# Moving the norm of the first batch half, its gates and one block product among the attention steps of a fused fp32 transformer kernel

## The chip, the cores and the metric

One core of a Trainium2 chip runs the whole program in one launch. The metric is device time in microseconds (us), the median of three runs. Five engines work side by side: TensorE (PE, matmuls and transposes), VectorE (DVE), ScalarE (ACT), GpSimd (POOL) and SyncE (SP), whose queue here issues most of the DMA transfers. Each executes its own instructions in order and waits on semaphores for the others.

## What is computed

The input `x` has 2 batch elements of 512 tokens with 1024 features; all arithmetic is fp32. Two layers follow, each with two residual steps:

```python
x = x + fake_quant_product(layernorm(x), ctx)        # layer 0
x = x + linear_with_mixed_lora(layernorm(x))         # layer 0
x = x + cross_attention(layernorm(x), ctx, ctx)      # layer 1: 32 heads, 8 kv heads, head size 128
x = x + ffn(layernorm(x))                            # layer 1
```

The cross attention has 1024 context positions, rotary embedding, a mask, a softmax and an output projection `wo` (4096 to 1024). The last step, which the change moves, is

```python
logits = h @ gate_w.T + expert_bias                  # h = layernorm(x), 4 experts
one_hot = jax.nn.one_hot(jnp.argmax(logits, -1), 4)
z = jnp.einsum('nh,erh->ner', h, lora_A)             # rank 8
delta = jnp.einsum('neh,ne->nh', jnp.einsum('ner,ehr->neh', z, lora_B), one_hot)
x = x + h @ W_up.T + delta
```

## The kernel before

The program is one long list of instructions written by Python generators; each `next()` emits a stretch of one of them, and that is how stages are interleaved. TensorE always runs in the order in which the program is written (L977). In the attention loop (L1123 to L1149) DVE, ACT and POOL do so too; behind it, and for SP throughout, a scheduler chooses the order. Tiles come from pools: `u8` (8 KB a partition, 14 buffers), `u4`, `u2`, `small` in SBUF; in PSUM `wide` with two buffers and `b` with four. A transfer or an operation into a tile waits until the earlier user of its buffer is done.

**Products.** The large products use one level of the Strassen-Winograd scheme: seven block products in place of eight, with sums of the operand blocks made before (`left_sums`, `right_sums`, L229 to L276, on DVE or, for attention's output, on POOL: L245 to L253; for weights L259, L262, L264, L267) and of the results after (`seven_onto`: L316, L317, L320 on DVE, L322 on POOL). The matmuls of all of them are recorded at L347.

**Attention.** `attention` (L836 to L927) takes one head per step, 64 heads (the first 32 belong to batch 0), with three phases a step that work on different heads:

- phase 0: scores of head n+2 (L748) and the addition of the mask by DVE (L762); loads of the next head's q and, every fourth step, of kT and v (`begin`) through SP;
- phase 1: the finished head is normalized by POOL (L822); every fourth step POOL forms the operand sums of a finished group of four heads; three or four stretches of the output projection of the group before (L347 with L317, L320, L322), which adds into the rows of `x`; the tree of maxima (L770 to L776);
- phase 2: the sum of the exponentials is turned (`turn_sum`, PE at L712, DVE at L714, L785), two halves of the product with v (`attend`, L811), and the exponentials of head n+1 (DVE L794, ACT L797, then POOL L800, L803, L804, L805, which add up the denominators).

The rows of `x` of one batch element lie in two 1 MB tiles (`halves`). They were stored to DRAM by `put_away` (L1087) earlier and are fetched again when the projection of that batch element begins (L873). Batch 0's projections end around step 36; its rows then lie unused until the last steps.

**The norm.** `all_moments` (L179) makes the statistics of a batch element, one quarter of 128 rows per `next` (BNStats, L163, and aggregation, L164), then one Sqrt on ACT (L186), then a reciprocal (L188). `scaled` (L166) subtracts and multiplies on DVE. `transposed` (L200) turns 128 rows: eight PE transposes into a `wide` PSUM tile (L204), two copies to SBUF by ACT (L205) and DVE (L206).

**Gates.** `gated` (L930) multiplies the turned rows with 36 columns (4 gate logits, 32 columns of `lora_A`): 8 matmuls for each of four quarters (L939), into two `b` tiles; each appears as two records in the profile. DVE then takes maxima and a mask per quarter (L950 to L957), POOL clears the tile for two quarters (L960), DVE multiplies (L962); PE turns the result (L972), DVE copies it (L973). It is the additional operand of four of the seven products of `linear` (L562).

**The end.** In the last five attention steps the statistics, scaling and turning of batch 0 are interleaved; the gates of batch 0 follow as one run of matmuls, the weights `W_up` are loaded and summed (`matrix`, L544), and the seven products of both row blocks follow, mixed with what is left of attention. Then batch 1 is normed among the last products of batch 0 (`weave`), its gates follow as one run, then its products and the stores of the output (L1171, L1180).

Of the kernel before, what the change touches and what calls it, by code (L numbers as in the profile page):

```python
# [39 lines left out]
def decoder_kernel(  # L40
# [300 lines left out]
    def advance(stretches, n):  # L341
        for _ in range(n):
            next(stretches)
# [585 lines left out]

    def gated(quarters):  # L930

        zT, diff = u2([P, S]), u2([P, 256])
        gaccs = []
        for t in range(NT):
            if t % 2 == 0:
                gacc2 = ps_b((P, 2, 256))
            gacc = gacc2[:, t % 2]
            for c in range(NC):
                nc.tensor.matmul(  # L939
                    gacc[:, :NGA],  # L940
                    chunk(quarters, c, t),
                    ga_t[:, c, :],
                    start=(c == 0),
                    stop=(c == NC - 1),
                )
            gaccs.append(gacc)
        zs = []
        for t, gacc in enumerate(gaccs):
# [12 lines left out]
            z = z2[:, t % 2]  # L961
            nc.vector.tensor_tensor(  # L962
                z[:, : E1 * R1].rearrange("p (e r) -> p e r", r=R1),
                gacc[:, E1:NGA].rearrange("p (e r) -> p e r", r=R1),
                lg.unsqueeze(2).to_broadcast([P, E1, R1]),
                ALU.mult,
            )
            zs.append(z)
        yield
        tr = ps_tr()  # L970
        for t, z in enumerate(zs):
            nc.tensor.transpose(tr[:, t, :], z, ident)  # L972
        nc.vector.tensor_copy(zT, tr.rearrange("p t n -> p (t n)"))  # L973
        yield split_tokens(zT, diff)
# [143 lines left out]
                w = quad_weights(wq, q + 1)  # L1118


    extra = {-2: 3, -1: 2, 0: 2, 1: 2, 2: 2, 3: 2, 4: 1}
    steps = attention({**extra, "products": main, "later": later})
    with tc.manual_schedule(  # L1123
        engines={
            mybir.EngineType.DVE,
            mybir.EngineType.Activation,
            mybir.EngineType.Pool,
        }
    ):
        for _ in range(3 * (B * NH - 5)):  # L1130
            next(steps)
        stats = all_moments(0)
        for _ in range(NT):
            for _ in range(2):
                next(steps)
            ready = next(stats)
            next(steps)
        next(steps)
        next(stats)
        next(steps)  # L1140
        next(stats)
        hs, norms = normed(0, u8, 2, ready)
        next(norms)
        next(steps)

    for _ in range(2):
        next(steps)
        for _ in range(2):
            next(steps)  # L1149
            next(norms)  # L1150
    gates = gated(hs)
    next(gates)
    for _ in range(2):
        next(steps)
    zTs = [next(gates), None]
    bl_t = u4([P, D])
    nc.sync.dma_start(bl_t, bl1T)
    w_ops = matrix(wupT, u8, 4)
    main = linear(0, token_sums(hs, lambda: u4([P, 4, 256])), w_ops, lambda: zTs[0], bl_t)
    advance(main, 4)  # L1160
    for _ in range(3):
        next(steps)
# [12 lines left out]
    advance(main, 2)  # L1175
    zTs[1] = next(gates)
# [75 lines left out]
```

## Time and profile before

| what | value |
|---|---|
| median of 3 runs | 2507.97 us (2507.82 to 2508.96) |
| the profiled execution | 2505.61 us |
| its span in the profile | 2503.8 us |
| mean granted TensorE clock | 0.989 |
| instructions | 19692 |
| attention step, start of scores to start of the next, four in mid-run | 21.55, 19.82, 21.92, 19.83 us |
| the same with the statistics in it, near the end | 22.47, 20.70, 22.33, 20.71 us |
| POOL's last addition to batch 0's rows ends | 1759.8 us |
| loads of kT, v, q around there are issued, and their data used | 1750.9 us, 1778.3 us |
| a 1 MB store of rows, and a 1 MB fetch, issue to landing | 3.9 us, 6.3 us |

How to read the profile: the row of busy shares gives each engine's busy time, the share of the span, and its records. A timeline line has the start, the length, the engine, the line of the kernel, the operation, the output and its inputs by pool, shapes, the count of like records in a row, and in brackets the idle time before it and who ended it. A row of waits has the engine and line that waited, the line waited for, the total, the count and the longest. A window row has the stretch, its length, busy time and records of each engine, the granted clock of TensorE (1.00 is full speed), the mean busy share of the DMA engines, and GB/s.

### The profile page before, as it was taken

Reading aid. Unit: us, or ns where it says so; the run is one execution under the profiler, and the core shown is the slowest. Engines: PE = TensorE matmul, PEld = TensorE weight load, DVE = VectorE, ACT = ScalarE, POOL = GpSimd, SP = SyncE. Lnnn points to the kernel's source line nnn. Section 1 sums busy time; section 2 is a strip of 40 time slices with the busy share of each in tenths; the row PEclk is TensorE's granted clock in tenths of the full one; section 3 lists DMA queues with packets and bytes.
Section 4 is the critical chain, followed back from the end, with each engine's and each line's share of the span. In section 5 each row is a group of like instructions: output and inputs, shape, how many; then the busy total and the mean of one; then the engine's idle time right before and its main releaser. Section 6 shows DMA issues by size and latency. Waiting matters only on the chain. (4 is left out here: it accounts for less than half of the span.)

```text
span 2503.8 us, 19692 instructions
## 1 busy us (share of the span) xinstructions
PE 2441.2 (97%) x6848; PEld 1218.0 (49%) x6856; DVE 1851.0 (74%) x2036; ACT 527.7 (21%) x615; POOL 1006.5 (40%) x536
## 2 busy tenths in 40 slices
PE   7999999999999998989999999999999999998998
PEld 3477458654444443434444444444444444444453
DVE  5848764346886547888888888888888888896451
ACT  1201221011122222222222222222222222223000
POOL 0000010111000001567677767776777667666121
PEclk8999999999999999999999999999999999999899
DMA  7225232013894221244323332443234323333100
GB/s 263 105 94 196 85 120 102 21 67 109 296 336 174 80 97 58 80 126 114 93 80 93 114 94 83 123 147 96 82 88 114 102 75 88 114 93 108 52 34 34
DMA packets 147379, 277.54 MB, mean 111 GB/s; under 512 B 29200, under 2 KB 47136, under 8 KB 146256
## 3 DMA queue, kind: packets, MB, share of 16 engines
q1 hardware_dynamic: 107024, 235.96, 28.1%
q10 hardware_dynamic: 39824, 39.60, 6.6%
q8 instruction: 55, 0.90, 0.1%
q0 software_dynamic: 432, 0.71, 0.1%
q14 instruction: 44, 0.36, 0.1%
HBM read 217.24 MB, written 58.98 MB: 110 GB/s over the span
## 5 line engine op out<-in xcount | busy, mean ns | idle before, releaser
L347 PE MATMUL b<-u,u 128*128 128x512 f32 (+1 forms) x3648 | 1416.6, 546 | 23.5 <-DVE u L291 10.0
L347 PEld LDWEIGHTS b<-u,u 128*128 128x128 f32 x3648 | 694.2, 192 | 710.8 <-issue 623.6
L748 PE MATMUL wide<-u,u 128*128 128x512 f32 x1024 | 455.3, 595 | 17.2 <-DVE small L714 8.5
L811 PE MATMUL b<-u,u 128*128 128x512 f32 x1024 | 461.3, 593 | 0.0
L800 POOL TENSOR_TENSOR u<-u 128x1024 f32<-128x1024 f32 x64 | 151.5, 2367 | 735.8 <-DMA row<-small 383.9
L762 DVE TENSOR_TENSOR u<-wide,u 128x1024 f32<-128x1024 f32 x256 | 312.7, 1224 | 129.0 <-PE wide L748 129.0
L797 ACT ACTIVATE u<-u 128x2048 f32<-128x2048 f32 x128 | 244.7, 1912 | 695.3 <-DVE u L794 633.9
L748 PEld LDWEIGHTS wide<-u,u 128*128 128x128 f32 x1024 | 193.0, 190 | 268.3 <-issue 175.4
L794 DVE TENSOR_TENSOR u<-u,b 128x2048 f32<-128x2048 f32 x128 | 290.3, 2268 | 0.0
L322 POOL TENSOR_TENSOR u<-u,u 128x512 f32<-128x512 f32 x120 | 185.5, 1564 | 228.3 <-DVE u L320 213.5
L811 PEld LDWEIGHTS b<-u,u 128*128 128x128 f32 x1024 | 186.7, 192 | 185.2 <-issue 185.2
L320 DVE TENSOR_TENSOR u<-u,b 128x512 f32<-128x512 f32 x200 | 135.9, 680 | 140.8 <-PE b L347 140.8
L803 POOL TENSOR_TENSOR u<-u,u 128x1024 f32<-128x1024 f32 x64 | 150.7, 2355 | 37.8 <-ACT u L797 37.6
L804 POOL TENSOR_TENSOR u<-u,u 128x1024 f32<-128x1024 f32 x64 | 150.8, 2356 | 4.9
L822 POOL TENSOR_TENSOR u<-u,u 128x512 f32<-128x512 f32 x64 | 119.8, 1871 | 16.0 <-DMA u<-row 16.0
L1054 POOL DMA_DIRECT2D u<-in_b_dram x1 | 0.6, 561 | 301.5 <-PE wide L450 301.5
L216 ACT ACTIVATE u<-u 64x512 f32<-64x512 f32 x72 | 45.2, 628 | 343.2 <-DVE u L293 166.9
L770 DVE TENSOR_TENSOR u<-u 128x1024 f32<-128x1024 f32 x64 | 115.6, 1806 | 0.0
L712 PEld LDWEIGHTS wide<-ident,u 128*128 128x128 f32 x512 | 80.4, 203 | 70.9 <-issue 56.6
L772 DVE TENSOR_TENSOR u<-u,u 128x1024 f32<-128x1024 f32 x64 | 105.8, 1654 | 0.2
L805 POOL TENSOR_TENSOR u<-u 128x512 f32<-128x512 f32 x64 | 100.2, 1566 | 4.9
L774 DVE TENSOR_TENSOR u<-u,u 128x1024 f32<-128x1024 f32 x64 | 97.0, 1515 | 0.2
(124 smaller groups left out, 1553.9 us busy)
## 6 DMA issues: line engine op xcount, KB each, us to landing
u<-row ACTq DMA_DIRECT2D x128, 256.0 KB, 3.7
u<-wo SPq DMA_DIRECT2D x64, 512.0 KB, 3.9
u<-in_wo_dram SPq DMA_DIRECT2D x48, 512.0 KB, 4.6
u<-in_wq_dram SPq DMA_DIRECT2D x32, 512.0 KB, 4.1
q<-u SPq DMA_DIRECT2D x64, 256.0 KB, 2.1
u<-in_wo_dram SPq DMA_DIRECT2D x16, 1024.0 KB, 7.9
wo<-u SPq DMA_DIRECT2D x32, 512.0 KB, 3.9
u<-q SPq DMA_DIRECT2D x64, 256.0 KB, 4.2
```

The lines of the kernel that those rows point to most:

```text
L320: nc.vector.tensor_tensor(c, c, acc, ALU.add)
L322: nc.gpsimd.tensor_tensor(c, c, u, ALU.add)
L347: nc.tensor.matmul(acc, lhsT, rhs, start=start and k == 0, stop=k == len(pairs) - 1, skip_group_check=True,)
L748: nc.tensor.matmul(sc[:, ts(n, HALF)], self.kT[:, ts(2 * j + n, P)], self.qT, start=True, stop=True,)
L762: nc.vector.tensor_tensor(self.e[j // 2][:, js, :], sc.rearrange("p (k q) -> p k q", k=2), mask[j], ALU.add)
L794: nc.vector.tensor_tensor(e, e, self.nmf.unsqueeze(1).to_broadcast([P, 4, S]), ALU.add)
L797: nc.scalar.activation(e, e, AF.Exp)
L800: nc.gpsimd.tensor_tensor(d, e[:, 0:2, :], e[:, 2:4, :], ALU.add)
L803: nc.gpsimd.tensor_tensor(d, d, e[:, 0:2, :], ALU.add)
L804: nc.gpsimd.tensor_tensor(d, d, e[:, 2:4, :], ALU.add)
L811: nc.tensor.matmul(self.acc, self.v[:, k, :], self.e[j][:, k % 4, :], start=(k == 0), stop=(k == NKT - 1),)
L822: nc.gpsimd.tensor_tensor(self.oT, self.oT, self.den, ALU.mult)
```

## The change

- The statistics of batch 0 move from steps 57 to 61 to steps 38 to 42 (`all_moments(0)`, one quarter in phase 1 of steps 38 to 41, the Sqrt in phase 0 of step 42, the reciprocal in phase 1).
- In step 42 the two row tiles of batch 0 are stored to DRAM through SP, and their buffers are given up; two `u8` tiles for the turned rows are taken.
- In steps 44 and 48 one half of the rows (1 MB) is fetched again into one `u8` tile; the four quarters are scaled in steps 45, 46, 49, 50 (in place, in the fetched tile) and turned in steps 46, 47, 50, 51.
- In step 61 two quarters of `W_up` are loaded, and the rows are fetched back. All gate matmuls of batch 0 stand in phase 1 of step 62, in one run, and write one `wide` PSUM tile in place of two `b` tiles; DVE's part and the loads of the other two weight quarters in phase 2; the turning of its result and the first of the seven products, for both row blocks, in phase 1 of step 63. The loop with a written-out order on DVE, ACT and POOL now runs to the end of step 63.
- `token_sums` and `right_sums` follow, then two phases of attention, then five more stretches of products.
- For batch 1 the gate matmuls of a quarter (8) stand directly behind the turning of the next quarter, and each such pair between products of batch 0, in place of one run of 32 after all four.

```diff
     def gated(quarters):
         zT, diff = u2([P, S]), u2([P, 256])
-        gaccs = []
+        gaccs = ps_wide().rearrange("p (t n) -> p t n", t=NT)
         for t in range(NT):
-            if t % 2 == 0:
-                gacc2 = ps_b((P, 2, 256))
-            gacc = gacc2[:, t % 2]
             for c in range(NC):
                 nc.tensor.matmul(
-                    gacc[:, :NGA],
+                    gaccs[:, t, :NGA],
...
                 )
-            gaccs.append(gacc)
+            yield
...
+    stats = all_moments(0)
+    last = {"zT": [None] * B, "w": [None] * 7, "h": [None] * 7}
+
+    def turn_away():
+        last["ready"] = next(stats)
+        put_away(0)
+        hs = [u8([P, 4, S]) for _ in range(2)]
+        last["hs"] = [[hs[ch][:, :, ts(th, 256)] for ch in range(2)] for th in range(2)]
+
+    def fetch_half(i):
+        last["rows"] = u8([P, 2, D])
+        nc.sync.dma_start(last["rows"], x_d[0][i])
+
+    def scale_row(t):
+        mean, rstd = last["ready"][t]
+        r = last["rows"][:, t % 2, :]
+        nc.vector.tensor_scalar(r, r, mean, rstd, ALU.subtract, ALU.mult)
+
+    def turn_row(t):
+        transposed(
+            last["rows"][:, t % 2, :],
+            [last["hs"][t // 2][j][:, :, ts(t % 2, P)] for j in range(2)],
+        )
...
+    def fetch_rows():
+        x[0] = halves()
+        for t, d in zip(x[0], x_d[0]):
+            nc.sync.dma_start(t, d)
+
+    def begin_map():
+        hs = last["hs"]
+        last["h"][:2] = hs[0]
+        last["gates"] = gated(hs)
+
+    hooks = {(42, 0): [lambda: next(stats)], (42, 1): [turn_away]}
+    for t in range(NT):
+        hooks[(38 + t, 1)] = [lambda: next(stats)]
+    for i in range(2):
+        n = 44 + 4 * i
+        hooks[(n, 2)] = [lambda i=i: fetch_half(i)]
+        hooks[(n + 1, 1)] = [lambda i=i: scale_row(2 * i)]
+        hooks[(n + 2, 1)] = [lambda i=i: turn_row(2 * i), lambda i=i: scale_row(2 * i + 1)]
+        hooks[(n + 3, 1)] = [lambda i=i: turn_row(2 * i + 1)]
+    hooks[(61, 2)] = [
+        lambda: fetch_weight(1, 0, 0),
+        lambda: fetch_weight(2, 1, 0),
+        fetch_rows,
+        begin_map,
+    ]
+    hooks[(62, 1)] = [lambda: advance(last["gates"], 4)]
+    hooks[(62, 2)] = [
+        lambda: next(last["gates"]),
+        lambda: fetch_weight(7, 0, 1),
+        lambda: fetch_weight(3, 1, 1),
+    ]
...
-        for _ in range(3 * (B * NH - 5)):
+        for i in range(3 * (B * NH + 2)):
             next(steps)
-        stats = all_moments(0)
-        for _ in range(NT):
-            for _ in range(2):
-                next(steps)
-            ready = next(stats)
-            next(steps)
...
-        hs, norms = normed(0, u8, 2, ready)
-        next(norms)
-        next(steps)
-
+            n, phase = divmod(i, 3)
+            for act in hooks.get((n - 2, phase), ()):
+                act()
+            if (n - 2, phase) == (63, 1):
+                zTs = [next(last["gates"]), None]
+                h_ops, parts = last["h"], last["w"]
+                w_ops = lambda i, c: parts[i - 1][:, c, :]
+                bl_t = u4([P, D])
+                nc.sync.dma_start(bl_t, bl1T)
+                main = linear(0, h_ops, w_ops, lambda: zTs[0], bl_t)
+                advance(main, 2)
...
-    gates = gated(hs)
-    next(gates)
-    for _ in range(2):
-        next(steps)
-    zTs = [next(gates), None]
-    bl_t = u4([P, D])
-    nc.sync.dma_start(bl_t, bl1T)
-    w_ops = matrix(wupT, u8, 4)
-    main = linear(0, token_sums(hs, lambda: u4([P, 4, 256])), w_ops, lambda: zTs[0], bl_t)
-    advance(main, 4)
-    for _ in range(3):
+    h_ops[:] = token_sums(last["hs"], lambda: u4([P, 4, 256]))
+    for _ in range(2):
         next(steps)
-    advance(main, 3)
+    parts[:] = right_sums(
+        nc.vector, parts[0], parts[6], parts[1], parts[2], lambda: u8([P, 4, HALF])
+    )
+    advance(main, 5)
     for _ in steps:
         pass
     hs, norms = normed(1, u4, 4)
-    weave(main, norms, 1, 2)
-    for _ in norms:
+    gates = gated(hs)
+
+    def turned_and_gated():
+        next(norms)
+        yield
+        next(norms)
+        yield
+        for _ in range(3):
+            next(norms)
+            next(gates)
+            yield
+        next(gates)
+        yield
+        next(gates)
+        yield
+
+    side = turned_and_gated()
+    weave(main, side, 1)
+    for _ in side:
         pass
     for t in range(NT):
         nc.sync.dma_start(out[0, ts(t, P), :], rows(0, t))
-    gates = gated(hs)
-    next(gates)
```

More of the change, by code (lines that the diff above doesn't have):

```diff
@@ L945, in gated @@
                 )
-            gaccs.append(gacc)
+            yield
         zs = []
-        for t, gacc in enumerate(gaccs):
+        for t in range(NT):
+            gacc = gaccs[:, t, :]
             lg = small([P, E1])
@@ L1122, in decoder_kernel, with fetch_weight @@
     steps = attention({**extra, "products": main, "later": later})
+    stats = all_moments(0)
[17 more added lines that the diff above has]
+        )
+    def fetch_weight(i, ch, nh):
+        t = last["w"][i - 1] = u8([P, 4, HALF])
+        nc.sync.dma_start(
+            t,
+            wupT[ts(ch, 4 * P), ts(nh, HALF)].rearrange("(c p) n -> p c n", p=P),
+        )
[8 more added lines that the diff above has]
+    hooks = {(42, 0): [lambda: next(stats)], (42, 1): [turn_away]}
+    for t in range(NT):
+        hooks[(38 + t, 1)] = [lambda: next(stats)]
[17 more added lines that the diff above has]
+    ]
     with tc.manual_schedule(
@@ L1129, in decoder_kernel @@
     ):
[L1130 removed]
+        for i in range(3 * (B * NH + 2)):
             next(steps)
[L1132 to L1144 removed]
+            n, phase = divmod(i, 3)
[10 more added lines that the diff above has]
+    h_ops[:] = token_sums(last["hs"], lambda: u4([P, 4, 256]))
     for _ in range(2):
         next(steps)
[L1148 to L1163 removed]
+    parts[:] = right_sums(
+        nc.vector, parts[0], parts[6], parts[1], parts[2], lambda: u8([P, 4, HALF])
+    )
+    advance(main, 5)
     for _ in steps:
```

## The prediction, made before the changed kernel was run

> **What bounds the kernel now.** I read the page's busy shares first, then PE's waits after 2150 us, then PE's timeline from 2280 us on, then windows cut at the clock's edges.
>
> ```profile
> PE 2441.2 (97%) x6848; PEld 1218.0 (49%) x6856; DVE 1851.0 (74%) x2036; ACT 527.7 (21%) x615; POOL 1006.5 (40%) x536
> ...
> PEclk8999999999999999999999999999999999999899
> ```
>
> TensorE is busy for 97% of the span and is the bound. A change that leaves its matmuls alone can only win where PE stands or where its clock falls. The clock row has two dips: at the start and in the third slice from the end (2316 to 2441 us), which this change rebuilds. The waits of PE there:
>
> ```profile
> PE wide L712 <- POOL u L805: 6.8, 1, 6.8
> PE b L972 <- DVE u L962: 5.9, 3, 3.2
> ...
> PE b L347 <- DVE u L267: 0.8, 1, 0.8
> ```
>
> PE's timeline shows where they stand and which groups take longer than the same group elsewhere:
>
> ```profile
> 2280.18 7.05 PE L347 MATMUL b<-u,u 128*128 128x512 f32 x16
> 2287.06 1.04 PE L204 MATMUL wide<-ident,u 128*128 128x128 f32 x8
> 2294.89 1.13 PE L712 MATMUL wide<-ident,u 128*128 128x128 f32 x4 [6.79 <-POOL u L805]
> 2295.81 8.06 PE L811 MATMUL b<-u,u 128*128 128x512 f32 x16
> ...
> 2311.09 7.03 PE L811 MATMUL b<-u,u 128*128 128x512 f32 x16
> 2317.96 1.04 PE L204 MATMUL wide<-ident,u 128*128 128x128 f32 x8
> 2318.83 7.91 PE L939 MATMUL b<-ga_t,u 128*128 128x36 f32 x64
> 2326.55 9.82 PE L347 MATMUL b<-u,u 128*128 128x512 f32 x16
> ...
> 2343.42 53.63 PE L347 MATMUL b<-u,u 128*128 128x512 f32 x118
> ...
> 2429.82 9.51 PE L939 MATMUL b<-ga_t,u 128*128 128x36 f32 x64
> 2439.13 9.85 PE L347 MATMUL b<-u,u 128*128 128x512 f32 x16
> ```
>
> Sixteen L347 take 7.05 us at 2280.18, but 9.82 and 9.85 behind the two gate bursts (L939): 2.8 us each. The windows (last two columns DMA share and GB/s, before them the clock) show why:
>
> ```profile
> 2318.36:2321.78 3.42, 3.42 (x34) 1.00 1.04 380
> ...
> 2325.18:2328.60 3.42, 3.42 (x11) 0.50 0.00 0
> 2328.60:2332.02 3.42, 3.42 (x6) 0.50 0.00 0
> ...
> 2434.41:2444.65 10.24, 10.24 (x31) 0.50 0.01 2
> ```
>
> PE is busy throughout and its clock is halved: the long run of narrow gate matmuls costs clock, not only standing does.
>
> **The losses at hand.** The wait for L805, 6.8; the slower L712 and L811 after it (1.13 against 0.64, 8.06 against 7.03), 1.5; behind gates(0), 2.8; three waits for L962, 5.9, and half clock after them (2345 to 2350 shows 0.59), 2.8; gates(1), 9.51 against 7.91 plus 9.85 against 7.05, 4.4. In all 24.2 us. The 0.8 for L267 stays.
>
> **Part 1: statistics, steps 57–61 to 38–42.** BNStats, aggregate, Sqrt, reciprocal are the same instructions. Step from one head's scores to the next's: 21.55, 19.82, 21.92, 19.83 us in mid-run, sum 83.1; 22.47, 20.70, 22.33, 20.71 with the statistics, sum 86.2. They cost 3.1 us because DVE is close to PE there (20.47 of 22.47). They move to four steps of the same kinds: 0 net, bounds ±1 (Sqrt's 1.28 us table load on ACT moves along).
>
> **Part 2: scaling and turning in steps 45–51.** Per 128 rows: 8 PE transposes, 0.87 us start to start (2317.96 to 2318.83), four times 3.5 us; 0.81 us DVE scaling; 0.69 us DVE copy; an ACT copy (ACT is busy 5 of 21 us). The transposes leave the tail (−3.5, inside the sum of part 4) and enter steps that PE fills: +3.5. DVE's cover: the step with four projection stretches has DVE at 19.03 of 21.55; 1.5 more is 20.5 of 22.4. The statistics put it at 20.47 too and cost 0.8 a step; here PE itself gains 0.87 of work, so I take +0.5 in all, bounds 0 and 3.1 (the statistics' price once more).
>
> **Part 3: transfers on SP.** Two 1 MB stores of batch 0's rows at step 42 (such a store takes 3.9 us to land), two fetches for the norm (6.3 us each), two to bring the rows back at step 61. SP takes its queue in order, and the stores stand ahead of kT, v and q of the next head. They wait for POOL's last add to batch 0's rows, at 1759.8, where the loads behind them are issued at 1750.9 now: 9 us, plus 8 for two stores, is 17 us of delay. Those loads are due at 1778.3, 27.4 us after their issue: cost 0. If the cover were gone, PE would stand by what exceeds it. Fetches follow their step's loads and have a whole step (20 us) until the scaling: 0. Of the rows' return the second half waits in SP's queue for a buffer that attention of head 62 frees; behind it stand only the last weight quarters, which by my order land some 10 us before they are due: 0, bounds 0 and 4 (a 1 MB transfer). POOL's queue is passed by no new instruction here. Nothing in this part can gain.
>
> **Part 4: the last steps, batch 0.** In the changed order the gates (32 instructions, 64 records) follow the projection that starts at 2280.18, at 2287.06, in the hole where PE waited 6.79 us for POOL. They take 7.7 us (2318.83 to 2326.55) to 9.3 (2429.82 to 2439.13): end G ≈ 2295.6. By then POOL has finished: it ended L805 at 2294.8 with two L322 and an L822, 1.26 each, queued ahead; in the changed order none of the three is, so L805 ends by about 2291. The wait for L805 goes.
>
> What is late next is the gate result. PE after G: L712 0.48, L811 6.87, twelve L347 5.16, and 2.7 of half clock left over from the burst: at the transposes of z (L972) by G+15.2. The vectors' way is longer. The turn_sum of head 62 is now behind the gates, and both exponentials of head 63 are behind it on DVE: reduce and reciprocal to G+1.4, L794 twice 4.5, exp 1.9, POOL's L803, L804, L805 2.36+2.36+1.26, with hand-overs G+14.3. On POOL the two memsets for z are behind those adds, and L962 needs them. So the first quarter's product is done at G+14.7, the other three at 1.5 each (the fourth quarter's chain ran alone from 2341.61 to 2343.1), up to 1.2 more where POOL's L822 is beside it (L954 took 1.24 us there against 0.23): G+20. PE waits 4.8 us at L972, with the first block products and everything of head 63 behind it. Bounds of that wait: 0, if the hand-overs overlap and the half clock is longer, and 8, if each DVE step runs beside POOL. I take 4.8, since POOL's and DVE's timelines have these durations.
>
> The transposes end at 2295.6+20.5 = 2316.1. Still to do of what was done at 2343.42: L712 0.48, L811 6.87, sixteen L347 6.88, 14.2 in all: 2330.3 against 2343.42, **−13.1**. Half clock after the wait: 1.7 (one window of 3.4 us at half speed; two would be 3.4) instead of 2.8: **−1.1**.
>
> **Part 5: batch 1's gates, 16 records (1.9 us) beside each quarter's transposes, among dense products.** The Trainium skill, "TensorE: Matmul & The Clock Gate", section "Why this matters for your kernels", asks only that PE be kept busy without gaps of some 3 us: then a burst of gates loses no clock and cutting it brings 0, the total −10. The row has PE busy 3.42 of 3.42 at 0.50, so the rule doesn't hold for this stream; I take the row. Against the cut speaks the same page's "Part 4: PE-mode transpose": transposes don't count as PE-busy in the same way, so that 0.87 us of them and 1.9 of gates together could drop the clock four times, 1.7 each: 6.8 lost instead of 4.4, total −7.7. But the window 2318.36:2321.78 holds 0.5 us of transposes and 2.9 of gates, and the clock in the next is still 1.00; it fell only after two such windows. A quarter fills at most 2.8 of one. I take the whole loss back: **−4.4**.
>
> **Sum.** −13.1 −1.1 −4.4 +3.5 +0.5 = −14.6 on the profiled execution of 2505.61 us (span 2503.8 and 1.8 around it): 2491.0. The median lies 2.36 above that execution, so 2493.4.
>
> **Rivals.**
> A, as summed: −11 to −17, 2491 to 2497. Chance 0.56.
> B, no new wait: the memsets or head 63's exponentials come earlier than I place them, PE reaches z at full clock: −14.6 −4.8 −1.7 = −21, with half of it −18: 2487 to 2490. For it: that head 63's exponentials stand behind the turn_sum is read from the order, and two of its steps may overlap. Against it: POOL's sums follow from measured durations. 0.18.
> C, the middle doesn't hide it or the cut gates still lose clock: with part 5 at 0 the sum is −10.2; with part 2 at its 3.1 besides, −7.6; with part 5 at +2.4 and part 2 at 3.1, −5.2. 2498 to 2503. For it: the statistics were not hidden either. 0.17.
> D, slower: SP's queue. Place: the stores at step 42 ahead of the next head's kT, v and q. It decides once their delay exceeds 27.4 us; to end slower by 5 us, PE must lose 19.6, so with 3.4 of clock lost the delay must reach 44, where I count 17. That takes stores that wait over a step longer than for the add at 1759.8: a step and a half more (32 us) is 22 of idle and 3.4 of clock, +11: 2519. Against it: nothing in POOL's order holds that add. 0.05.
> E, it doesn't do what it says: the gates don't fill the hole but wait for the fetched and turned rows or for a PSUM tile, so that the hole of 6.8 and the slow 1.5 after it stay and the gates' 7.7 come on top of them: −14.6+6.8+1.5+7.7 = +1.4, 2509. The rows are ready ten steps earlier, which speaks against it. 0.04.
>
> **How the numbers follow.** Median measurements here tell about 0.2%, 5 us, from no change: 2503 to 2513 is "same". A, B and most of C are faster: 0.88. The rest of C and E are "same": 0.07; D 0.05. Range: A with B below and C above to 2502, leaving out the far end of C, E and D; from 2486, a little below B's −21.
>
> **What would show it.** In the changed profile: L712 with no wait for L805 beside a gate burst at about 2290 (plus 4 from the middle); one wait at L972 of 3 to 6 us for L962, with the memsets behind L805 on POOL; clock 0.50 behind gates(0) but 1.00 through batch 1's norm; steps 45 to 51 longer by 0.9 to 1.1 each where turned rows lie; no wait of L748 for loads around step 42. I am wrong if L748 waits for DMA at steps 42 to 50, if the clock dips four times after 2400 us, or if L972 doesn't wait at all.

## The result, and the profile after

| | before | after |
|---|---|---|
| median | 2508.47 us (6 runs, 2507.01 to 2513.34) | 2494.1 us (6 runs, 2491.7 to 2498.1) |
| profiled execution | 2505.61 us | 2491.89 us |
| its span | 2503.8 us | 2490.1 us |

The ratio of the runs is 0.994, 95% interval 0.993 to 0.995: 14.4 us less by the medians, 13.7 by the profiled executions. The prediction was 2493.4. (The ratios given for the experiments below are each to the kernel before, run beside that experiment; its median lay between 2509.0 and 2510.1 us there.) The first lines of the page after, busy time and (second) TensorE's clock in 40 slices:

```profile
PE 2434.2 (98%) x6848; PEld 1214.5 (49%) x6856; DVE 1852.5 (74%) x2036; ACT 527.9 (21%) x615; POOL 1011.8 (41%) x536
...
PEclk8999999999999999999999999999999999999999
```

The dip near the end is gone from the clock row, and PE's busy time is 7 us shorter for the same 6848 matmuls: that part is clock; the rest of the 13.7 us is standing time. PE's waits after 1700 us:

```profile
PE b L971 <- DVE u L961: 5.1, 4, 1.8
PE wide L712 <- POOL u L805: 1.7, 1, 1.7
...
PE b L347 <- DVE u L267: 0.8, 1, 0.8
```

(L971 and L961 are L972 and L962 of before; the gates, L939, are now L937.) The 6.8 us for L805 shrank to 1.7, and those 1.7 stand in another place, in step 45. The wait for the product of z was 5.9 and is 5.1. PE's timeline of the last steps:

```profile
2286.26 7.03 PE L347 MATMUL b<-u,u 128*128 128x512 f32 x16
2293.13 9.19 PE L937 MATMUL wide<-ga_t,u 128*128 128x36 f32 x64
2302.13 1.09 PE L712 MATMUL wide<-ident,u 128*128 128x128 f32 x4
2303.01 7.97 PE L811 MATMUL b<-u,u 128*128 128x512 f32 x16
...
2317.45 0.33 PE L971 MATMUL b<-ident,u 128*128 128x128 f32 x1 [1.31 <-DVE u L961]
...
2322.74 8.35 PE L347 MATMUL b<-u,u 128*128 128x512 f32 x16
...
2338.26 50.80 PE L347 MATMUL b<-u,u 128*128 128x512 f32 x118
```

The gates stand where the hole was; the L712 behind them waits for nothing, but is about as slow as behind the hole in before (1.09 us, 1.13 there), and part of L811 (7.97) and of the first product behind z (8.35) ran at a lower clock: mean 0.88 and 0.84. At 2338.26 PE has done what it had done at 2343.42 before.

**Where the time went, by stretches.** The stretch ahead of attention's first step, which the change leaves alone, differs by up to 8 us between the profiled executions of all the kernels here (first step at 934.4 to 942.3 us). So kernels are compared below by stretches of their traces, each from one start of a group of matmuls to another; steps 36 to 61 mostly repeat to 0.02 us where they hold the same work; now and then one differs by up to 0.4.

| stretch | before | after | difference |
|---|---|---|---|
| ahead of step 38, the change not in it | | | +0.8 |
| steps 38 to 43 (statistics come) | 124.49 | 126.85 | +2.4 |
| steps 44 to 52 (scaling, turning, fetches) | 188.19 | 194.17 | +6.0 |
| step 53 to the last projection's 16 matmuls (statistics go) | | | −3.1 |
| from there to the 118 L347 in a row | 63.24 | 52.00 | −11.2 |
| those, to the wait for L267 | 54.47 | 51.64 | −2.8 |
| from there to the end (gates of batch 1) | 105.91 | 100.20 | −5.7 |

### The profile page after: what moved, and what is told of

Same layout as the page of the kernel before. It is cut to its first block, busy times and chain, and to the rows that moved or that the text cites. A ratio compares the mean times of both kernels' runs of the same rounds, so it can differ in the third digit from the quotient of the medians.

```text
span 2490.1 us, 19684 instructions
## 1 busy us (share of the span) xinstructions
PE 2434.2 (98%) x6848; PEld 1214.5 (49%) x6856; DVE 1852.5 (74%) x2036; ACT 527.9 (21%) x615; POOL 1011.8 (41%) x536
## 4 chain that ended last, share of the span: by engine, by line
PE 59%; DVE 7%; POOL 2%; issue 2%; DMA 1%; ACT 1%; SPq 0%; POOLq 0%; DVEq 0%; ACTq 0%
PE b L347 26%; PE wide L748 15%; PE b L811 15%; PE wide L712 2%; DVE u L794 2%; DMA u<-in_wo_dram 1%; PE wide L937 1%; DVE u L772 1%; DVE u L774 1%; DVE small L714 1%; POOL u L804 1%; POOL u L803 0%; DVE u L762 0%; DVE u L222 0%; DVE u L219 0%
## 5 line engine op out<-in xcount | busy, mean ns | idle before, releaser
L347 PE MATMUL b<-u,u 128*128 128x512 f32 (+1 forms) x3648 | 1408.6, 543 | 25.3 <-DVE u L291 10.8
L347 PEld LDWEIGHTS b<-u,u 128*128 128x128 f32 x3648 | 691.4, 191 | 707.5 <-issue 619.4
L811 PE MATMUL b<-u,u 128*128 128x512 f32 x1024 | 461.2, 593 | 0.0
L800 POOL TENSOR_TENSOR u<-u 128x1024 f32<-128x1024 f32 x64 | 151.6, 2369 | 747.4 <-DMA row<-small 385.0
L811 PEld LDWEIGHTS b<-u,u 128*128 128x128 f32 x1024 | 186.7, 192 | 185.2 <-issue 185.2
L803 POOL TENSOR_TENSOR u<-u,u 128x1024 f32<-128x1024 f32 x64 | 150.8, 2356 | 35.6 <-ACT u L797 34.6
L712 PEld LDWEIGHTS wide<-ident,u 128*128 128x128 f32 x512 | 80.2, 204 | 64.6 <-issue 54.7
L805 POOL TENSOR_TENSOR u<-u 128x512 f32<-128x512 f32 x64 | 102.0, 1594 | 5.0
```

What stands on the lines that cost most here:

```text
L347: nc.tensor.matmul(acc, lhsT, rhs, start=start and k == 0, stop=k == len(pairs) - 1, skip_group_check=True,)
L800: nc.gpsimd.tensor_tensor(d, e[:, 0:2, :], e[:, 2:4, :], ALU.add)
L803: nc.gpsimd.tensor_tensor(d, d, e[:, 0:2, :], ALU.add)
L811: nc.tensor.matmul(self.acc, self.v[:, k, :], self.e[j][:, k % 4, :], start=(k == 0), stop=(k == NKT - 1),)
```

## The experiments

Sizes near 1 us could not be told from medians, whose 95% intervals reach 2 to 4 us to either side; the verdicts rest on the stretches wherever both are given.

**cut_alone: before, with batch 1's gates cut.**

```diff
-        gaccs = []
+        gaccs = ps_wide().rearrange("p (t n) -> p t n", t=NT)
...
-    weave(main, norms, 1, 2)
-    for _ in norms:
+    gates = gated(hs)
...
+    side = turned_and_gated()
+    weave(main, side, 1)
+    for _ in side:
...
-    gates = gated(hs)
-    next(gates)
```

> The kernel before with only one part of the change: batch 1's gate matmuls cut into four quarters, each behind the turning of the next quarter, among the last products of batch 0. Everything else of the tail stays as before. Theory (a run of 64 narrow gate matmuls loses the clock, a quarter of them does not): 4.4 us less by the sum of the prediction, 5.7 by what the changed kernel showed between the last weight sum and the end; the profile has no half clock after the gates of batch 1, the half clock after gates of batch 0 stays. About 2503 to 2504 us beside 2508. Rival (the narrow matmuls cost the same wherever they stand; the gain came from elsewhere): 0 within 1 us. Second rival (the transposes beside them drop the clock four times): 2 to 3 us more.

Measured 2509.77, ratio 0.9999 (0.9991 to 1.0007): nothing gained in all. But the last stretch fell from 105.9 to 100.9, as the theory had it. The loss lay in front: I had taken over the changed `gated` as a whole, so that batch 0's gates too wrote one PSUM tile for all quarters, and the wait of L971 grew from 5.9 to 10.8 us. So this run doesn't isolate the cut; cut_clean does.

**cut_clean: the same, with batch 0's gates left as before.**

```diff
+    def gated_cut(quarters):
...
-    weave(main, norms, 1, 2)
-    for _ in norms:
+    gates = gated_cut(hs)
...
-    gates = gated(hs)
-    next(gates)
```

> The kernel before with batch 1's gates cut into quarters and nothing else: batch 0's gates keep their two b tiles of PSUM, which the earlier run with this cut had put into one wide tile (its batch 0 wait for z grew from 5.9 to 10.8 us). Theory: from the end of the wait for the last weight sum to the end of the program it gains 5.0 us as in that run, and with nothing lost in front of it the whole gains 4.4 to 5.0: 2503 to 2504 beside 2508.5. Rival (the cut really brings nothing): 2508, or the time comes back elsewhere.

Measured 2505.01, ratio 0.9981 (0.9972 to 0.9989), which is 4.8 us; the last stretch 100.93. The cut gives 5.0, and PE's waits are those of before.

**one_run: after, with batch 1's gates in one run again.**

```diff
-    weave(main, side, 1)
+    weave(main, norms, 1, 2)
...
+    gates = gated(hs)
+    advance(gates, NT + 1)
```

> The changed kernel with only that part taken back: batch 1's gates in one run of 64 records after the norm, as before. Theory: 4.4 to 5.7 us more than the changed kernel, 2498 to 2500 us, with about 10 us of half clock behind the run. Rival: as the changed kernel, 2494.

Measured 2496.97, ratio 0.9953 (0.9941 to 0.9964); the last stretch 103.63, which is 3.4 more than after: the right direction, less than expected. The run of 64 took 7.97 us, and the 16 L347 behind it 9.76. The same run of 64 took between 7.91 and 10.95 us in all these traces: the clock falls somewhere inside it or behind it, and the loss moves by 1 to 2 us with the place. In after, from its start (2293.13) to the twelve L347 (2310.82), PE needed 17.7 us, in clear_on_dve 17.8; in one_run, later_fetch and rows_on_act, with the same order there, 19.3. So a difference under 1.6 us tells nothing where such a run stands in the stretch. In after, batch 1's quarters keep the clock:

```profile
2293.13:2302.13 9.00, 9.00 (x66) 0.77 0.17 31
...
2401.60:2435.85 34.25, 34.25 (x147) 1.00 0.12 46
```

(PE only; the clock is the number before the last two.) The first row is batch 0's run, the last the whole stretch with turnings, quarters of gates and products: full clock.

**clear_on_dve: after, with z's tiles cleared by DVE.**

```diff
-                nc.gpsimd.memset(z2, 0.0)
+                nc.vector.memset(z2, 0.0)
```

> The changed kernel with the tiles for z cleared by DVE in place of POOL. Nothing else. In the changed kernel DVE waits 4.0 us for POOL's clearing, which stands behind the sums of head 63, and PE then waits 5.1 us in four pieces for the products of z (L971 for L961). Theory (the chain gates, sums on POOL, clearing, product of z sets the end of that wait): the first product comes 3.5 us earlier, the last about 3, and TensorE's wait falls to 1 to 2.5 us: 2.5 to 4 us less, about 2491. Rival (DVE's own small steps beside POOL, 1.9 us each for L953 and L956, set it): under 1 us less.

The wait that the prediction had named is in after's DVE timeline:

```profile
2308.83 1.91 DVE L953 TENSOR_SCALAR small<-small,small 128x4 f32<-128x4 f32 x1
...
2311.17 2.01 DVE L956 TENSOR_SCALAR small<-small,small 128x4 f32<-128x4 f32 x1
2317.20 0.19 DVE L961 TENSOR_TENSOR u<-wide,small 128x32 f32<-128x32 f32 x1 [4.02 <-POOL u L959]
```

and POOL's beside it:

```profile
2308.36 2.36 POOL L800 TENSOR_TENSOR u<-u 128x1024 f32<-128x1024 f32 x1 [7.56 <-ACT u L797]
2310.80 2.36 POOL L803 TENSOR_TENSOR u<-u,u 128x1024 f32<-128x1024 f32 x1
...
2316.86 0.56 POOL L959 MEMSET u<- 128x256 f32 x2
```

Without that wait of DVE, PE's wait at L971 fell from 5.1 to 2.9, a little more than I expected to be left, and from the last projection to the 118 L347 it took 49.5 us instead of 52.0. The median, 2493.7 (ratio 0.9934, 0.9919 to 0.9949), doesn't show it. So both are true. The clearing behind POOL's sums set the wait: counted from the turn_sum, the first product of z came 3.7 us earlier without it. And DVE's small steps on 128x4 numbers, 0.23 us alone and up to 2.0 beside POOL's sums, took half of that back: more of them now ran beside those sums (1.64, 0.93 and 0.70 us), and the last product came only 1.7 us earlier.

**gates_behind: after, with batch 0's gates behind the turn_sum and the product with v of head 62.**

```diff
-    hooks[(62, 1)] = [lambda: advance(last["gates"], 4)]
...
-        lambda: next(last["gates"]),
+        lambda: advance(last["gates"], 5),
```

> The changed kernel with batch 0's gate matmuls behind the turn_sum and the product with v of head 62 instead of in front of them. Nothing else. TensorE then waits again for POOL's L805 in front of that turn_sum. By the sum of the prediction, with the changed kernel's times: that wait is only 2.8 us now (TensorE is free at 2293.1, L805 ends at 2295.9), because POOL's L322 are no longer ahead; head 63's exponentials and sums start 6 us earlier and the clearing of z no longer stands in the way of the product; the last product of z comes about 2 us earlier than now: 1 to 2.5 us less than the changed kernel from the projection at 2286.26 to the turned z. Rival (filling the hole with the gates is what won there): 3 to 5 us more.

```profile
2288.66 7.03 PE L347 MATMUL b<-u,u 128*128 128x512 f32 x16
2298.33 1.12 PE L712 MATMUL wide<-ident,u 128*128 128x128 f32 x4 [2.64 <-POOL u L805]
...
2307.35 9.50 PE L937 MATMUL wide<-ga_t,u 128*128 128x36 f32 x64
...
2324.63 0.60 PE L971 MATMUL b<-ident,u 128*128 128x128 f32 x4
```

The hole is back, 2.64 us long, and the wait for z is gone: the four L971 run as one. The stretch to the 118 L347 takes 50.6 us against 52.0 in after (53.6 in one_run, later_fetch and rows_on_act). Median 2491.63, ratio 0.9929 (0.9917 to 0.9941). Up to the turned z there was no gain (36.4 us against 36.5, the half clock took it); the 1.4 came after it. The rival falls: filling the hole with the gates didn't pay, and this put the attribution of the whole gain in question.

**norm_alone: the changed middle and batch 1's cut, batch 0's gates and products in the order of before.**

```diff
-    hooks[(62, 1)] = [lambda: advance(last["gates"], 4)]
...
-        for i in range(3 * (B * NH + 2)):
+        for i in range(3 * B * NH):
...
+    for _ in range(6):
+        next(steps)
+    hs = last["hs"]
+    gates = gated(hs)
+    next(gates)
     for _ in range(2):
         next(steps)
...
+    zTs = [next(gates), None]
```

> The changed kernel with its middle (statistics, scaling and turning of batch 0 in steps 38 to 51, rows put away and fetched) and its cut gates of batch 1, but batch 0's gates, weights and products in the order of before: gates in one run at the very end of attention, two b tiles of PSUM. It tells what the move of the norm is worth by itself. From the start of the projection's last 16 matmuls (2280.18 before) to the turned z it took 63.2 us before. Theory by terms: the four turnings leave it (3.5), the wait for L805 goes from 6.8 plus 0.9 of turning to about 4.0, because without the norm POOL no longer has two L322 ahead of that sum: 56 to 57.5 us; with the middle's 6.0 and the cut's 5.0, the whole is 4 to 6 us under before: 2503 to 2505. Rival (the hole stays as it was): 60 to 61 us, the whole 1 to 2 under before. Second rival (the norm's move is what the change gains): as the changed kernel, 14 under before.

Measured 2491.82, ratio 0.9929 (0.9916 to 0.9943): my expectation of 2503 to 2505 was wrong by 12 us, and the second rival holds. PE's timeline:

```profile
2284.63 7.03 PE L347 MATMUL b<-u,u 128*128 128x512 f32 x16
2296.78 1.13 PE L712 MATMUL wide<-ident,u 128*128 128x128 f32 x4 [5.13 <-POOL u L805]
...
2319.17 8.61 PE L985 MATMUL b<-ga_t,u 128*128 128x36 f32 x64
2327.59 9.09 PE L347 MATMUL b<-u,u 128*128 128x512 f32 x16
2336.52 0.60 PE L1018 MATMUL b<-ident,u 128*128 128x128 f32 x4
2336.95 50.81 PE L347 MATMUL b<-u,u 128*128 128x512 f32 x118
```

The hole is there, 5.13 us, and the half clock behind the gates; but all four turnings of z (L1018, the L972 of before) follow without a wait, at full clock after it. The stretch takes 52.32 us, the next 51.64: against before 13.75 less, where after has 14.07 less. **With the norm gone, the place of the gates and of the first product is worth 0.3 us beside after, and nothing beside the three kernels of after's order that took 53.6; that is within the 1.6 us. The norm's leaving is worth the rest of these 14 us.** By terms it is 3.5 of turnings, 1.4 of the hole (6.79 against 5.13 and 0.26), 5.9 of waits for L962, and 2.8 of half clock behind them, 13.6 in all. Why the waits went is in DVE's timeline. Before:

```profile
2312.50 0.17 DVE L785 RECIPROCAL small<-small 128x4 f32<-128x4 f32 x1
2320.33 0.69 DVE L206 COPY u<-wide 128x512 f32<-128x512 f32 x1 [7.67 <-ACT u L205]
...
2322.61 1.23 DVE L245 TENSOR_TENSOR u<-u,u 128x1024 f32<-128x1024 f32 x1
```

and in norm_alone:

```profile
2313.23 0.18 DVE L785 RECIPROCAL small<-small 128x4 f32<-128x4 f32 x1
2313.33 1.20 DVE L245 TENSOR_TENSOR u<-u,u 128x1024 f32<-128x1024 f32 x1
```

DVE waited 7.67 us for the last turned quarter, with the operand sums for the product (L245), which read it, behind that copy; these then fell among the small steps of the gates. Without the norm three of the four sums are done while PE still multiplies with v, and the 3.4 us L259, which split the gate steps before, starts only after the last z. The order is the scheduler's, so this is what the traces show and not a thing that I took apart singly. norm_alone has the whole middle of the change and the cut of batch 1's gates in it, so its median shows the two together, not the norm's move alone.

**later_fetch: after, with the fetches of rows one phase later, scaling and turning one step later.**

```diff
-        n = 44 + 4 * i
-        hooks[(n, 2)] = [lambda i=i: fetch_half(i)]
+        n = 45 + 4 * i
+        hooks[(n, 0)] = [lambda i=i: fetch_half(i)]
```

> The changed kernel with the two 1 MB fetches of batch 0's rows put from the last phase of steps 44 and 48 to the first phase of steps 45 and 49, scaling and turning one step later. Nothing else. In the changed kernel step 45 is 2.0 us and step 49 0.6 us longer than before, with a wait of 1.7 us of the turn_sum (L712) for POOL (L805). Theory: the fetch stands in the DMA engines when the 2 KB row of maxima is stored, its landing takes 5.3 us in place of 2.9, ACT's queue waits with the second exponential behind it, and POOL is late. With the fetch after those rows the wait goes: 2.0 to 2.6 us less than the changed kernel, about 2491.7. Rival (DVE's scaling and turning are what the steps cannot hide): the same time as the changed kernel, the wait for L805 in the steps where the scaling is now (46, 50).

Measured 2492.45, ratio 0.9933 (0.9921 to 0.9945). Steps 44 to 53 are 0.8 us shorter than in after (213.2 against 214.0; 0.4 of it came back in step 54), less than expected, for a reason that the trace tells: SP's order is the scheduler's, and it issued the first fetch at the same place as before. Only the second was really later, behind the row's store: there ACT issued the row's broadcast 2.6 us after the store, not 6.1, and step 49 took 19.83 us without any wait. Step 45 took 20.74 with no scaling in it. Neither theory was tested cleanly, but the 0.9 us that step 45 lost here are not DVE's scaling.

**rows_on_act: after, with scaling and both copies by ACT.**

```diff
-        nc.vector.tensor_scalar(r, r, mean, rstd, ALU.subtract, ALU.mult)
+        nc.scalar.activation(r, r, AF.Identity, bias=mean, scale=rstd)
```

(`mean` made −mean·rstd by four small DVE operations.)

> The changed kernel with batch 0's rows scaled by ACT (scale and bias per row, bias made by four small DVE operations) and both copies of each turned quarter made by ACT: DVE has 6.0 us less to do in steps 45 to 51. Nothing else. The changed kernel's steps 44 to 52 take 194.2 us, 6.0 more than before, of which TensorE's own transposes are 3.5. Theory (DVE is what these steps cannot hide): 191.7 to 192.2 for the nine steps, 2.0 to 2.5 us less. Rival (the fetches and their collisions with the small row stores make it): 193.5 to 194.5 as now. Second rival (ACT's exponentials come late behind the new work): over 195.

Steps 44 to 52 took 195.9 us, longer, not shorter; median 2493.17, ratio 0.9936 (0.9924 to 0.9949). Step 45 alone took 24.5, 2.7 more than in after:

```profile
1944.62 0.75 PE L712 MATMUL wide<-ident,u 128*128 128x128 f32 x4 [2.73 <-POOL u L805]
1945.21 5.30 PE L811 MATMUL b<-u,u 128*128 128x512 f32 x8
```

That looks like the second rival, but it isn't ACT's new work: the scaling (L1141) started at 1939.70, behind the exponential that was late (1934.66), and the fetch, issued as in after, took 9.6 us to land, not 8.4. PE waited 1.0 us longer than in after and then lost 1.7 us of clock (0.67 over the L811, 5.30 us in place of 3.60). Steps 46 to 52 took 149.9 us against 150.8, and the turning steps, 46, 47, 50 and 51, each 0.89 more than before: TensorE's turnings (0.87). So DVE's part was about 1 us, and a cost of ACT's work was not seen.

**fetch_alone: before, with six added 1 MB fetches that nothing reads.**

```diff
+            if (n - 2, phase) in ((8, 2), (12, 2), (16, 2), (21, 1), (25, 1), (29, 1)):
+                nc.sync.dma_start(u8([P, 2, D]), x_d[0][0])
```

> The kernel before with six added fetches of 1 MB of rows into a tile that nothing reads, in the steady middle: in the last phase of steps 8, 12 and 16 (as the change has them in 44 and 48) and after the projection of steps 21, 25 and 29. Nothing is scaled or turned. It measures the fetch by itself. Theory (collision with the store of the 2 KB row, behind which ACT's queue waits): steps 9, 13 and 17, 19.83 us now, take 0.3 to 0.9 longer each, the row's store lands after about 5 us instead of 2.9; steps 21, 22, 25, 26, 29, 30 are unchanged within 0.1. Rival (fetches cost nothing, DVE's scaling makes the stall): all at 19.83 and 21.54.

Measured 2515.99, ratio 1.003 (1.0018 to 1.0041), slower by about 7 us. With the steps beside them the six cost 6.65 us, 1.1 each, 0 to 2.0. The half of the expectation on a later place failed as a test: SP issued all six 5.8 us ahead of steps 9, 13, 17, 21, 25 and 29, each 19.83 us before. In order of what they cost:

| step | fetch, issue to landing | ACT's store of the row, issue to landing | the step |
|---|---|---|---|
| 29 | 7.2 us | 4.9 us | 19.83 us |
| 21 | 7.7 | 6.1 | 20.16 |
| 17 | 8.3 | 6.0 | 20.79 |
| 25 | 8.5 | 6.8 | 21.82 |
| 13 | 8.5 | 6.2 | 21.82 |
| 9 | 8.6 | 6.4 | 21.83 |

The later the fetch lands, the longer the step; why it lands at different times isn't known. PE's waits in 1150 to 1650, a stretch with none before:

```profile
PE wide L712 <- POOL u L805: 5.7, 4, 1.7
```

And the two transfers and ACT's timeline about step 9, which show the way there:

```profile
u<-x SPq DMA_DIRECT2D x1, 1024.0 KB, 8.6
row<-small ACTq DMA_DIRECT2D x1, 2.0 KB, 6.4
```

```profile
1174.41 0.33 ACTq L721 DMA_DIRECT2D row<-small  x1
...
1180.80 0.33 ACTq L727 DMA_DIRECT2D u<-row  x1
...
1181.65 1.91 ACT L797 ACTIVATE u<-u 128x2048 f32<-128x2048 f32 x1 [3.15 <-DVE u L762]
```

ACT stores a 2 KB row, and issues its broadcast only when the row has landed. The fetch was issued by SP at 1171.97 and landed at 1180.6, the store at 1180.8, 6.4 us after its issue; in step 9 of before it took 4.7, in step 45 it went from 3.2 to 6.6 in after. (The 2.9 and 5.3 of the expectations are medians that mix this store with the ones behind it.) Behind the broadcast, in ACT's order, stands the second exponential of a head, whose input DVE had finished 2.3 us before; behind that POOL's sums; behind those TensorE's turn_sum. The Trainium skill, "DMA: Bandwidth & Descriptors", section "Queues, rings and completion order", has a rule that would make a small store late though it has a queue of its own: the semaphore write comes only after all earlier writes of that DMA engine, across its queues. The traces agree: in all six cases the store landed 0.2 us behind the fetch. No run here takes that apart from plain sharing of the engines.

The same happened in norm_alone, at the end: there the first fetch of the returning rows was issued at 2280.95, the row's store at 2281.10, and the store landed after 5.5 us, half a microsecond behind the fetch. POOL's L803 began 4.3 us after L800, in gates_behind 2.9. So about 1.4 us of the 5.13 us hole of norm_alone is this collision and has nothing to do with the order of the gates.

**early_gates: after, with batch 0's gates in quarters in steps 53 to 56, the first product in the hole, the later fetches.**

```diff
+    for t in range(NT):
+        hooks[(53 + t, 1)] = ([lambda t=t: turn_gate(t - 1)] if t else []) + [lambda t=t: gate_quarter(t)]
+    hooks[(53 + NT, 1)] = [lambda: turn_gate(NT - 1)]
+    hooks[(62, 1)] = [lambda: advance(nonlocal_main["main"], 2)]
```

> The changed kernel with batch 0's gates taken out of the end altogether: each quarter's 8 matmuls and its maxima and mask in steps 53 to 56, its turning one step later, cleared by DVE; the first block product for both row blocks in step 62, where the run of gates was; the fetches one phase later. If the sums stand, this takes from the end the run of gates (9.0), the half clock behind it (about 2.7), the wait for the products of z (5.1) and the half clock after that (1.3), and adds to the middle 7.7 us of matmuls at full clock and 1 to 3 for DVE: 6 to 9 us less than the changed kernel, 2485 to 2488. Rival (the steps of the middle lose to DVE's extra operations what the end gains): 2492 to 2496. Second rival (the run of gates only hid a wait that comes back as a wait for L805): 2 to 3 us less.

Measured 2483.73, ratio 0.9903 (0.9888 to 0.9918): faster than before and after. It bundles four changes to after: the gates in the middle, z cleared by DVE, the first product in step 62 and the later fetches. PE's timeline:

```profile
2292.89 13.90 PE L347 MATMUL b<-u,u 128*128 128x512 f32 x32
...
2320.99 0.75 PE L712 MATMUL wide<-ident,u 128*128 128x128 f32 x4 [1.72 <-POOL u L805]
...
2328.45 50.80 PE L347 MATMUL b<-u,u 128*128 128x512 f32 x118
```

The stretch to the 118 L347 falls from 52.0 to 35.6 us, 16.4 less; steps 53 to 57 grow from 102.95 to 111.57, 8.6, of which the matmuls moved there are 7 to 7.5. Net 7.8, inside the expected 6 to 9; one 1.7 us wait for L805 remains, and step 56 has a new one of 1.0 us for DVE. What each of the four changes gave isn't taken apart.

**early_gates_act: the same, with both copies of a turned quarter by ACT.**

```diff
-        transposed(
...
+        for j in range(2):
+            nc.scalar.copy(last["hs"][t // 2][j][:, :, ts(t % 2, P)], tr[:, 4 * j : 4 * j + 4, :])
```

> The kernel with batch 0's gates in steps 53 to 56 (early_gates), and both copies of each turned quarter by ACT instead of one by DVE: 2.8 us less for DVE in steps 47 to 52, the scaling stays on DVE. Nothing else. Theory (DVE's extra work is part of what these steps cannot hide): steps 46 to 53, 172.7 us in early_gates, fall by 0.8 to 1.5; the time about 1 us under early_gates, 2482 to 2483. Rival (the excess is in the scaling alone or in transfers): no change, or later exponentials behind ACT's copies make it longer by up to 1.

Measured 2483.91, ratio 0.9902 (0.9888 to 0.9916). Steps 46 to 53 took 172.9 us against 172.6, so nothing was gained; step 45, which has nothing but the fetch, took 21.86 this time (20.59 in early_gates), with the same order: the fetch landed after 8.7 us, not 8.1. The copies are not the excess, and a fetch costs a different amount in each execution.

**early_gates_fetch: early_gates, with the fetches issued by ACT behind its row stores.**

```diff
-        nc.sync.dma_start(last["rows"], x_d[0][i])
+        nc.scalar.dma_start(last["rows"], x_d[0][i])
```

> The kernel with batch 0's gates in steps 53 to 56 (early_gates), with the two 1 MB fetches of rows issued by ACT, whose order is written out, behind the row stores and broadcasts of steps 45 and 49; SP, whose order the scheduler chooses, had issued them ahead of these stores in most runs. Nothing else. Theory (a fetch in front of the row's store costs 0 to 2.0 us, on average 1.1, by the six added fetches): steps 44+45 and 48+49, 41.76 and 41.75 in the kernel before, stay within 0.3 of that, less the 0.4 that step 44 loses in any case; together with the turning of the quarters steps 44 to 53 come to 213 to 214 us (214.8 in early_gates, 216.3 with ACT's copies), the median 0.5 to 1.5 under early_gates, 2482 to 2483.5. Rival (any 1 MB transfer there delays the rows, whoever issues it): one or both of steps 45 and 49 over 20.5, no gain; the broadcast beside it lands late and the exponentials of the next head with it.

ACT's timeline about step 45:

```profile
1921.95 0.33 ACTq L721 DMA_DIRECT2D row<-small  x1
...
1925.58 0.33 ACTq L727 DMA_DIRECT2D u<-row  x1
1926.00 0.39 ACTq L721 DMA_DIRECT2D row<-small  x1
...
1929.83 0.33 ACTq L727 DMA_DIRECT2D u<-row  x1
...
1930.27 0.36 ACTq L1134 DMA_DIRECT2D u<-x  x1
```

Steps 45 and 49 took 19.83 us each, steps 44 to 53 213.8; median 2482.61, ratio 0.9895 (0.9878 to 0.9912), the fastest kernel of this study, though its lead of a microsecond over early_gates is only shown in the steps. That supports the collision: the same transfers, in the same steps, cost nothing when they start behind the rows. Place and queue changed together here, but step 49 of later_fetch, early_gates and early_gates_act, where SP issued the fetch behind the row's stores, also took 19.83: it is the place.

## Why the prediction was right, and where it was not

The time was right to 0.7 us, the total better than its parts. That is in part luck: part 2 and 3 missed by 2.0 one way, part 5 by 1.3 the other, and in three of the five kernels with after's order of the end (one_run, later_fetch, rows_on_act) the gates' clock loss was 1.6 us larger than in after.

- **Part 1, statistics: 0 ± 1.** They cost 2.4 in steps 38 to 43 and left 3.1 behind at the end: −0.7. Right.
- **Part 2, +3.5 and +0.5.** Steps 44 to 52 grew by 6.0, not 4.0. TensorE's 3.5 was right. With the fetches out of the way (early_gates_fetch) the steps 44 to 53 are 213.8 against 208.0 + 3.5 + 1.8 for the gate quarter in step 53: 0.5 left for DVE (rows_on_act: about 1). Also right; the missing 2.0 belong to part 3.
- **Part 3, "Fetches follow their step's loads ...: 0."** This is the step that failed. I asked only whether the fetched rows come in time, not what else is on its way when they travel. A fetch costs 1.1 us on average, through ACT's queue; two make the 2 (step 45 alone lost 2.0, step 49 0.6). The stores, for which I had counted 17 us of delay, did as predicted: they were issued at 1760.63, kT behind them landed some 16 us later than in before, and PE didn't wait.
- **Part 4, −13.1 and −1.1.** Measured −11.2 and −2.8: −14.1 for −14.2, the half clock only lying in the other stretch. The new wait was 5.1 (4.8 predicted), its mechanism, L961 for the clearing behind POOL's sums, was there with 4.0 us on DVE, and clear_on_dve took 2.2 of the 5.1 away. But the text credits the gates' new place, "in the hole where PE waited 6.79 us". norm_alone shows that the order of before, without the norm, has the same 14 us within the spread. The sum was right because it was made from the instructions that stand in the changed order, and the norm was gone from it; the reason was wrong. The gates' place took away one hole and one clock loss and made a wait and a clock loss of the same size.
- **Part 5, −4.4.** The cut alone gave 5.0 in the stretch (cut_clean, 4.8 by the ratio), the changed kernel 5.7, and taking it back cost 3.4 (one_run). The rule that part 5 quotes doesn't hold for these narrow matmuls here (clock 0.77 over the run, with PE busy throughout by its records), and turnings beside 1.9 us of gates didn't drop the clock (1.00 over 34 us). Two slips: the second dip of the clock row, one slice, is 2316 to 2379 us, and four drops of the clock would have made −7.8, not −7.7; neither enters the sum.
- **Rivals.** C's loss in the middle appeared, by another cause; B's missing wait didn't. D and E had no sign: the loads of the next head were in time, and the gates filled the hole.

Left open: how much of a late landing is sharing and how much is order of completion; why one fetch lands after 7.2 us and the next after 8.6 with the same order; and which of the DVE operations that went first is worth most in norm_alone.

## What to carry to other kernels

When a change moves one thing out of a crowded place and rearranges what is left, build the removal alone: here the removal, with the cut of batch 1's gates, had the whole gain, and the rearrangement of this change only turned one wait into another (early_gates, another rearrangement, did gain). Cost a transfer not only by whether its data come in time but by what small, urgent transfer it may stand in front of, and put it, on a queue whose order you write, behind that one. Look at the clock behind a long run of narrow matmuls: here the whole run lost clock at every place that was tried, also among dense matmuls, and pieces of 1.87 us among dense ones lost none, at the end (clock 1.00 over 34 us) and in steps 53 to 56 of early_gates (1.00 in each).

## What the runs showed of the hardware

- A run of 64 records of 128x36 matmuls took 7.9 to 10.95 us in these traces, with no idle time of TensorE inside; 16 of them at a time among dense work, 1.87 each time in after.
- DVE's operation on 128x4 numbers with a scalar operand took 0.23 us alone, 1.91 and 2.01 beside POOL's additions, and ended each time 0.02 us after the addition did (L953 and L956 with L800 and L803 in after).
- With a 1 MB fetch (8.4 us to landing) issued 2 us ahead of it on another queue, a 2 KB store landed after 6.6 us in place of 3.2 in step 45 of the changed kernel, 0.2 us behind the fetch, and the step took 21.82 us in place of 19.83.
